# Three moves in a fused attention kernel: beta added to the residual's copy in DRAM, layer 0's product ahead of attention times v, and the projection always in a two-bank tile

## The chip, the core and the metric

The kernel runs on one core of one Trainium2 chip. The metric is the device time of a run in microseconds (us). All runs quoted are "fast" (no disturbed clock). PE is TensorE, DVE is VectorE, ACT is ScalarE, POOL is GpSimd, SP is SyncE; PEld in the profile is PE's weight load. SBUF is the on-chip memory that holds the kernel's tiles, PSUM the one into which PE writes its products (in this program in banks of 128 x 512 floats), DRAM the memory that holds inputs and outputs.

## The reference

The input x holds 128 blocks of 128 x 512 floats. There are two layers, each followed by a layer norm; cut to what matters:

```python
# layer 0: x[b] (128 x 512), adj (128 x 128), bias per row.
# With W1 = W2 = adj the gnn reduces to relu(max over columns of (adj @ x + b)) per row.
x = layernorm(x + L0(x, adj, adj, b0))
# layer 1: 8 heads of 64, masked with adj == 0
q, k, v = split(x @ w_qkv)
attn = softmax(where(adj == 0, -inf, q @ k.T * 64 ** -0.5))
o = (attn @ v) @ w_proj + b_proj
x = layernorm(x + o + layernorm(o) * gamma + beta)
```

## The kernel before

The 128 blocks are worked on in 32 groups of four. A period has two parts: the dense part (q and k of the group, transposed; PE alone sets the pace) and the attention part, in which PE does four times, for one block each: transposes of the softmax weights (`ppt`), scores of the present group (`psc`), the transposes of the next group's x (`ptx`), attention times v of the last group (`pav`), the output projection, a product for v (`pm`/`pd`), and layer 0's product of the group after next (`pa`). Dense products are done in three pieces: a float is split into a high part (rounding on ACT, mask on DVE), a low part and a correction, `x_h`, `x_l`, `x_d`; attention's output likewise into `oh`, `ol`, `od`.

The parts that the change touches:

```python
ps_1 = ctx.enter_context(tc.tile_pool(name="ps_1", bufs=4, space=bass.MemoryType.PSUM))  # one bank each
ps_2 = ctx.enter_context(tc.tile_pool(name="ps_2", bufs=2, space=bass.MemoryType.PSUM))  # two banks each

def conv(b):                       # layer 0's product
    ...
    pa[b] = ps_1.tile([P, D], FP, tag="ps1", name=f"pa_{b}")
    nc.tensor.matmul(pa[b], adjT, xs[b], start=True, stop=True)

def split(key, src, dsts):         # src is ptx or pav, in PSUM
    fh, fl, fd = dsts
    xh = work.tile([P, KC, P], FP, tag="xh", name=f"xh_{key}")
    nc.vector.tensor_scalar(xh.bitcast(I32), src.bitcast(I32), HIGH, None, op0=ALU.bitwise_and)
    hs[key] = fh, xh
    nc.vector.tensor_tensor(fl, src, xh, op=ALU.subtract)        # the last reader of src
    nc.vector.scalar_tensor_tensor(fd, fl.bitcast(FP), -HALF, xh, op0=ALU.mult, op1=ALU.add)

def product(key, two, terms):
    if two:
        pp = ps_2.tile([P, 2, D], FP, tag="ps2", name=f"pp_{key}")
        pm, pd = pp[:, 0, :], pp[:, 1, :]
    else:
        pm = ps_1.tile([P, D], FP, tag="ps1", name=f"pm_{key}")
        pd = ps_1.tile([P, D], FP, tag="ps1", name=f"pd_{key}")
    ...                            # 8 matmuls into pm, 4 into pd

def attention(g, t, starts):       # the order of PE and ACT is that of these places
    for i in range(G):
        u = t + starts[i]
        ...                        # now: group g, last: g - 1, nxt: g + 1, far: g + 2
        last(0.0, transpose_e)
        last(1.0, weights_T)
        now(0.95, scores)
        now(2.1, masked)
        now(3.5, row_max)
        ...
        nxt(2.0, transpose_x)
        nxt(2.5, split_x)
        ...
        u += 2.5
        if g < NG - 1:
            last(0.0, attend)
            u += 1.0
        if i and 0 < g:
            projection((g - 1) * G + i - 1, u)
            u += 2.8
        ...
        last(0.1, heads)
        last(0.8, lambda b: split_high(("o", b)))
        if 0 < g != NG - 1 and i < G - 1:
            dense_step(min(g, NG - 1), i + 1, u)
            u += 2.8
        far(-20.0, load_x)
        far(0.0, conv)
        far(1.0, conv_max)
        ...
```

The order on PE and ACT is given by hand, as these places; that on DVE and POOL is chosen by the scheduler of the program builder.

## Time and profile before

| | before |
|---|---|
| time, median of 3 runs | 2110.77 us (2108.1 to 2110.89) |
| span of the profiled run | 2108.8 us, granted clock 0.992 |
| up to the dense part of group 2 | 141.9 us |
| groups 2 to 29, 28 periods | 1802.5 us, median period 64.31 us, late groups 1.8 us |
| group 30 | 61.5 us |
| from the dense part of group 31 to the end | 102.9 us |

The time is from the first session; the comparison further down has one run more, hence 2110.83 us there. The rows after the second are cut from the trace by the start of the first dense matmul of each group. A "late group" is one whose period is over 0.05 us above the median; the sum is what the 28 periods take over 28 medians (rounded to 0.01 us, so it is good to some 0.2 us). The prediction shows the lines of the profile and how they are read; two groups of the page that it quotes only as numbers are these (line of the program, engine, operation, output and input tile, shapes, count; then busy us and mean ns of one; then idle time ahead of them and what ended most of it):

```profile
L420 ACT ACTIVATE o<-o,sum 128x512 f32<-128x512 f32 x128 | 104.0, 813 | 148.2 <-POOL sum L406 147.7
L360 POOL DMA_DIRECT2D xb<-in_L_gnn_ln_beta_dram x128 | 118.8, 928 | 203.8 <-DMA xb<-x 185.6
```

ACT stands 147.7 us behind small norm steps of POOL, and POOL stands 185.6 us behind loads of the residual (`xb`), because it may add beta to it only when it has landed.

### The profile page before, as it was taken

The page shows a single profiled execution, that of the slowest core. Times are in us where ns is not written, and L with a number is a line of the kernel's source. Part 1 is how long each engine was busy: PE and PEld are TensorE (multiplying, and loading weights), DVE is VectorE, ACT ScalarE, POOL GpSimd, SP SyncE. Part 2 cuts the span into 40 slices and gives each one's busy share as a digit, 9 for nine tenths or more (in the row PEclk, how much of TensorE's full clock was granted, in tenths as well). Part 3 has the DMA queues.
Part 4 walks back from the last instruction along what each step waited for, and adds up shares of the span by engine and source line. Part 5 has one row for each costly group of instructions (what it writes and reads, how often), then busy time and mean ns, then how long its engine had stood idle before and what let it go on. Part 6 is the DMA issues. An engine that isn't in the chain of part 4 may idle for free. (4 is left out here: it accounts for less than half of the span.)

```text
span 2108.8 us, 35003 instructions
## 1 busy us (share of the span) xinstructions
PE 2053.4 (97%) x12033; PEld 1599.1 (76%) x12033; DVE 1613.3 (77%) x2615; ACT 1458.4 (69%) x4130; POOL 734.8 (35%) x1329
## 2 busy tenths in 40 slices
PE   7899999999999999999999999999999999999997
PEld 5677777777777777777777777777777777777775
DVE  7787777887777877778877778777788777788777
ACT  5766676776767766767667677667677676776665
POOL 2123333323433333333234332333332343333345
PEclk9999999999999999999999999999999999999998
DMA  6224444445544345444455443444444444434444
GB/s 186 65 66 125 126 124 108 97 113 131 129 106 110 97 125 127 124 104 99 114 130 129 107 109 97 126 127 124 104 100 114 130 131 108 108 101 109 116 106 115
DMA packets 134433, 240.64 MB, mean 114 GB/s; under 512 B 14704, under 2 KB 18928, under 8 KB 134256
## 3 DMA queue, kind: packets, MB, share of 16 engines
q1 hardware_dynamic: 97680, 172.27, 25.2%
q0 software_dynamic: 36288, 66.08, 18.8%
q8 instruction: 95, 1.56, 0.3%
q14 instruction: 82, 0.67, 0.1%
q10 hardware_dynamic: 288, 0.07, 0.0%
HBM read 138.74 MB, written 67.11 MB: 98 GB/s over the span
## 5 line engine op out<-in xcount | busy, mean ns | idle before, releaser
L317 ACT ACTIVATE e<-e,nmax 128x128 f32<-128x128 f32 x1024 | 396.6, 391 | 3.8 <-DVE nmax L310 3.8
L380 POOL DMA_DIRECT2D xb<-o x124 | 112.9, 910 | 686.9 <-DVE o L385 593.5
L336 ACT COPY eT<-ppt 128x1024 f32<-128x1024 f32 x128 | 129.4, 1011 | 123.6 <-PE ppt L332 123.5
L420 ACT ACTIVATE o<-o,sum 128x512 f32<-128x512 f32 x128 | 104.0, 813 | 148.2 <-POOL sum L406 147.7
L398 POOL TENSOR_TENSOR sum<-sum,mhalf 128x1 f32<-128x1 f32 (+1 forms) x291 | 198.2, 681 | 22.3
L403 POOL TENSOR_SCALAR sum<-sum 128x1 f32<-128x1 f32 x256 | 140.8, 550 | 169.1 <-DVE o L385 167.1
L385 DVE SCALAR_TENSOR_TENSOR o<-o,sum,xb 128x512 f32<-128x512 f32 x128 | 95.7, 747 | 135.0 <-POOL sum L398 131.2
L317 ACT ACTIVATION_READ_ACCUMULATOR e<-e,nmax 128x1 f32 x1024 | 193.9, 189 | 0.0
L391 ACT ACTIVATE square<-o,sum 128x512 bf16<-128x512 f32 x256 | 183.4, 716 | 11.8 <-DVE o L385 9.8
L360 POOL DMA_DIRECT2D xb<-in_L_gnn_ln_beta_dram x128 | 118.8, 928 | 203.8 <-DMA xb<-x 185.6
L412 DVE SCALAR_TENSOR_TENSOR o<-o,sum,gamma_sb 128x512 f32<-128x512 f32 x128 | 95.9, 749 | 100.1 <-ACT square L391 95.3
L397 POOL TENSOR_SCALAR sum<-sum 128x1 f32<-128x1 f32 (+1 forms) x291 | 106.9, 368 | 187.5 <-ACT square L391 174.1
L332 PEld LDWEIGHTS ppt<-ident,e 128*128 128x128 f32 x1024 | 120.6, 142 | 51.8 <-issue 46.6
L302 DVE SCALAR_TENSOR_TENSOR e<-psc,mask 128x1024 f32<-128x1024 f32 x128 | 156.1, 1219 | 3.9 <-PE psc L295 3.9
L326 DVE TENSOR_TENSOR e<-e,sums 128x1024 f32<-128x1024 f32 x128 | 154.8, 1210 | 1.1
L310 DVE TENSOR_REDUCE nmax<-e 128x8 f32<-128x1024 f32 x128 | 154.7, 1209 | 0.0
L295 PE MATMUL psc<-qkT 64*128 64x128 f32 x2048 | 150.3, 286 | 2.8 <-DVE qkT L284 2.7
L170 PE MATMUL pa<-xt,adjT 128*128 128x512 f32 x256 | 133.9, 609 | 12.3 <-PE pd_(15, 1)_9801 L252 0.6
L295 PEld LDWEIGHTS psc<-qkT 64*128 64x128 f32 x2048 | 125.0, 188 | 26.9 <-issue 18.4
L345 PE MATMUL pav<-eT,v 128*64 128x128 f32 x2048 | 140.2, 279 | 2.1 <-ACT eT L336 2.1
L332 PE MATMUL ppt<-ident,e 128*128 128x128 f32 x1024 | 133.7, 274 | 0.0
L345 PEld LDWEIGHTS pav<-eT,v 128*64 128x64 f32 x2048 | 109.2, 136 | 24.8 <-issue 22.1
(4778 smaller groups left out, 5563.5 us busy)
## 6 DMA issues: line engine op xcount, KB each, us to landing
xt<-in_x_dram SPq DMA_DIRECT2D x128, 256.0 KB, 2.8
x<-xt SPq DMA_DIRECT2D x128, 256.0 KB, 3.6
xb<-x SPq DMA_DIRECT2D x128, 256.0 KB, 2.8
xb<-in_L_gnn_ln_beta_dram POOLq DMA_DIRECT2D x128, 256.0 KB, 4.4
o<-in_L_gnn_b_proj_dram SPq DMA_DIRECT2D x128, 256.0 KB, 3.8
out_dram<-o SPq DMA_DIRECT2D x128, 256.0 KB, 3.3
xb<-o POOLq DMA_DIRECT2D x124, 256.0 KB, 3.5
wraw<-in_L_gnn_w_qkv_dram SPq DMA_DIRECT2D x12, 256.0 KB, 4.2
```

Of the source, the lines that this page charges most:

```text
L170: nc.tensor.matmul(pa[b], adjT, xs[b], start=True, stop=True)
L295: nc.tensor.matmul(psc[:, s, hp, :], qkT[hs, hp, i, :], qkT[hs, KC + hp, i, :], start=True, stop=True,)
L302: nc.vector.scalar_tensor_tensor(e, pscs.pop(b).rearrange("p s a m -> p (s a) m"), scale, mask_b, op0=ALU.mult, op1=ALU.add,)
L310: nc.vector.tensor_reduce(nmax, es[b], AX.X, ALU.max, negate=True)
L317: nc.scalar.activation(e[:, j, :], e[:, j, :], AF.Exp, bias=nmax[:, j : j + 1], accum_out=sums[:, j : j + 1],)
L326: nc.vector.tensor_tensor(e, e, sums[:, :, None].to_broadcast([P, H, P]), op=ALU.mult)
L332: nc.tensor.transpose(ppts[b][:, j, :], e[:, j, :], ident)
L336: nc.scalar.copy(eTs[b], ppts.pop(b))
L345: nc.tensor.matmul(pavs[b][s * HD : (s + 1) * HD, hp, :], v[:, h * HD : (h + 1) * HD], eT[:, s * HP + hp, :], start=True, stop=True,)
L391: nc.scalar.activation(square, x, AF.Square, bias=s[:, 0:1], scale=-float(D), accum_out=s[:, 1:2],)
L398: nc.gpsimd.tensor_tensor(s, s, mhalf[:, :n], op=ALU.pow)
L403: nc.gpsimd.tensor_scalar(s[:, 2:3], s[:, 0:1], -1.0 / D, None, op0=ALU.mult)
```

## The change

The intent has three parts, called A, B and C from here on. **A**: layer 0's product moves from the end of a block to just ahead of attention times v. **B**: the projection of a group's first block gets a two-bank tile like the others. **C**: beta is added by a DMA to the residual's copy in DRAM, long before that copy is loaded again, rather than to the loaded copy in SBUF; the last step of the norm moves half a place later.

```diff
--- before.py
+++ after.py
@@ -208,6 +208,10 @@
         x1s[b] = dram.tile([P, D], FP, tag="x1", name=f"x1_{b}")
         nc.sync.dma_start(x1s[b], xs[b])
 
+    def beta_0(b):
+
+        nc.gpsimd.dma_start(x1s[b], row(ln_beta), accum_op=ALU.add)
+
     def transpose_x(b):
         g, i = divmod(b, G)
         pts[b] = ps_1.tile([P, KC, P], FP, tag="ps1", name=f"ptx_{b}")
@@ -352,16 +356,12 @@
         split(("o", b), pavs.pop(b), oTs[b])
 
     def residual(b):
-
         xbs[b] = work.tile([P, D], FP, tag="xb", bufs=3, name=f"xb_{b}")
         nc.sync.dma_start(xbs[b], x1s.pop(b))
 
-    def residual_beta(b):
-        nc.gpsimd.dma_start(xbs[b], row(ln_beta), accum_op=ALU.add)
-
     def project(b):
         parts = [*zip(oTs.pop(b), proj_forms)]
-        product(("o", b), b % G != 0, lambda kc: [(f[:, kc, :], w[:, kc, :]) for f, w in parts])
+        product(("o", b), True, lambda kc: [(f[:, kc, :], w[:, kc, :]) for f, w in parts])
 
     def bias(b):
         os[b] = work.tile([P, D], FP, tag="o", bufs=4, name=f"o_{b}")
@@ -434,7 +434,6 @@
     def normed(b, u, v, w, z):
 
         at(u - 14.0, residual, b)
-        at(u - 10.0, residual_beta, b)
         at(u - 4.0, residual_o, b)
         at(u, stats, b, 1)
         at(v, norm_1, b)
@@ -466,6 +465,10 @@
             nxt(2.5, split_x)
             nxt(3.3 if i == 3 else 5.0, split_high)
             u += 2.5
+            if g + 2 < NG:
+                far(0.0, conv)
+                far(0.9, conv_max)
+                u += 0.9
             if g < NG - 1:
                 last(0.0, attend)
                 u += 1.0
@@ -481,8 +484,6 @@
                 dense_step(min(g, NG - 1), i + 1, u)
                 u += 2.8
             far(-20.0, load_x)
-            far(0.0, conv)
-            far(1.0, conv_max)
             if NG - 1 <= g:
                 v = u + 8.9 if g == NG else u + 12.5 + 2.0 * i
                 normed((g - 1) * G + i, v, v + 1.5, v + 3.1, v + (8.6 if g == NG else 5.6))
@@ -512,12 +513,13 @@
                 v = u + (14.0 + 1.5 * i if g == 0 else (17.0, 21.0, DENSE + 4.0, DENSE + 12.0)[i])
                 at(v, norm_0, b + i)
                 at(v + 1.0, keep_0, b + i)
+                at(v + 25.0, beta_0, b + i)
         for i in range(G):
             if g > 0:
                 at(t + 6.0 + 3.0 * i, weights, (g - 1) * G + i)
             if g > 1:
                 u = t + (3.0, 7.5, 12.0, DENSE + 2.0 if g < NG - 1 else 16.0)[i]
-                normed((g - 2) * G + i, u, u + 3.5, u + 7.0, u + 10.5)
+                normed((g - 2) * G + i, u, u + 3.5, u + 7.0, u + 11.0)
 
 
     for b in range(G):
@@ -531,6 +533,7 @@
         at(u + 4.5, rstd_0, b, 1)
         at(u + 6.0, norm_0, b)
         at(u + 7.0, keep_0, b)
+        at(30.0 + b, beta_0, b)
         at(u + 7.0, transpose_x, b)
         at(u + 8.2 + 0.7 * b, split_x, b)
         at(u + 8.9 + 0.7 * b, split_high, b)
```

## The prediction

> **What bounds the kernel now.** I read the page's engine shares first, then busy time by stretches, then the timeline of one steady period of TensorE (PE) and VectorE (DVE), then the waits of PE. PE leads:
>
> ```profile
> PE 2053.4 (97%) x12033; PEld 1599.1 (76%) x12033; DVE 1613.3 (77%) x2615; ACT 1458.4 (69%) x4130; POOL 734.8 (35%) x1329
> ```
>
> The kernel works on 32 groups of four blocks. From the first matmul of one group's dense part to that of the next the timeline shows 64.3 us for nearly every group, and two neighbouring periods in the view by stretches are equal to the last digit (columns: span, then busy us of PE, PEld, DVE, ACT, POOL, granted clock, DMA share, GB/s):
>
> ```profile
> 1237.00:1301.30 64.30, 63.80 (x379) 49.79 (x377) 49.36 (x81) 44.92 (x129) 22.85 (x41) 1.00 0.45 115
> 1301.30:1365.60 64.30, 63.80 (x379) 49.79 (x377) 49.36 (x81) 44.92 (x130) 22.83 (x41) 1.00 0.45 115
> 1301.90:1329.70 27.80, 27.80 (x121) 22.28 (x120) 14.85 (x28) 20.76 (x55) 15.65 (x30) 1.00 0.48 120
> 1329.70:1365.10 35.40, 34.90 (x255) 26.96 (x254) 33.41 (x51) 23.06 (x72) 7.18 (x11) 1.00 0.43 115
> ```
>
> The reader is to see that PE has no idle time in the dense part (third line) and 0.5 us in the attention part (fourth), where DVE is busy 33.4 of 35.4 us. So time is PE's own work plus what DVE makes it wait in the attention part. The two places are in PE's timeline of that period (start, duration, then in brackets the idle time before):
>
> ```profile
> 1335.33 1.10 PE L252 MATMUL pd_(20, 1)_12966<-w_d,x_d 128*128 128x512 f32 x4
> 1336.83 1.10 PE L170 MATMUL pa<-xt,adjT 128*128 128x512 f32 x2 [0.40 <-PE pd_(20, 1)_12966 L252]
> ...
> 1343.41 1.09 PE L252 MATMUL pd_('o', 76)_13062<-p_d,od 128*128 128x512 f32 x4
> 1344.60 0.47 PE L249 MATMUL pm_(20, 2)_13084<-w_h,x_h 128*128 128x512 f32 x1
> ```
>
> Starts are safer than modelled ends. From pd's start to pa's is 1.50 us; four 128x512 matmuls at the 0.233 us spacing seen between them elsewhere take 0.93, so 0.57 us is a stall. From pd('o', 76) to pm(20, 2) is 1.19 us, so 0.26 us. After each the next start comes 0.08 us late as well (pa's second at 0.504 instead of 0.428; pm's at 0.31 instead of 0.233). Sum: 0.57 + 0.26 + 0.16 = 0.98 us a period. The releaser named is PE's own last matmul, which cannot be the reason: PE does not depend on it. DVE's timeline shows the reason:
>
> ```profile
> 1334.33 0.68 DVE L224 TENSOR_SCALAR xh<-ptx 128x512 int32<-128x512 int32 x1
> 1334.92 1.21 DVE L310 TENSOR_REDUCE nmax<-e 128x8 f32<-128x1024 f32 x1
> 1336.05 0.68 DVE L226 TENSOR_TENSOR x_l<-ptx,xh 128x512 fp32r<-128x512 f32 x1
> ...
> 1343.77 0.68 DVE L226 TENSOR_TENSOR x_l<-ptx,xh 128x512 fp32r<-128x512 f32 x1
> ```
>
> The first x_l ends at 1336.73 and pa starts at 1336.83; the second ends at 1344.45 and pm(20, 2) starts at 1344.60. x_l is the last reader of ptx (transposed x), and the one-bank PSUM pool has four buffers in rotation: in the first block of a period the order of allocation is ptx, pav, pm, pd, pa, so pa gets ptx's bank; in the second ptx, pav, pm('o'), pd('o'), pm(20, 2), so pm gets ptx's bank. The built program's semaphore waits say the same: both wait for DVE's x_l. PE's waits show the first stall once in each of the groups 2 to 29, 28 times, with 0.4 us idle (0.6 where something came late):
>
> ```profile
> PE pa L170 <- PE pd_(21, 1)_13599 L252: 0.4, 1, 0.4
> PE psc L295 <- DVE qkT L284: 2.7, 2, 1.8
> ```
>
> The second line is two extra waits (0.92 us in group 15's scores, 1.8 at the end): the period of group 15 is 65.67 us and of group 7 64.77, so 1.36 + 0.46 = 1.8 us of late arrivals in this run.
>
> **What the Trainium skill says.** "Perfetto Trace Analysis", section Optimization Strategy: consistent bubbles on the engine that should be saturated can mean there is too little SBUF or PSUM for the next tile. The trace agrees: 0.57 us, once a period, 28 times. Same page, Tensor Engine Instruction: the matmul's end is an estimate; agreed, the records overlap (pm's matmuls take 0.40 us and start 0.233 apart), hence I count by starts. "TensorE: Matmul & The Clock Gate", The mechanism: matmuls run in strict program order; so one waiting pa holds everything behind it, as the transposes ppt, which follow at 0.93 us, show. "DMA: Bandwidth & Descriptors", SWDGE vs HWDGE vs iDMA: accumulating in a DMA is for GpSimd-issued DMAs alone; so both versions keep beta's transfer on POOL (0.93 us per issue).
>
> **The change part by part.**
>
> (1) Layer 0's product (pa) ahead of attention times v. I listed the built programs' order on each engine. Per block PE now runs ppt, psc, ptx, pa, pav, projection, dense v. No matmul is added. With (2) the one-bank order is ptx, pa, pav, pm, pd in each of the first blocks: five tiles over four buffers, so pd takes ptx's bank, and later pa takes pm's, pav takes pd's, and so on. DVE's order moves too: xh(ptx), pa's maximum, x_l, then the row maximum (1.21 us), so x_l no longer stands behind it. For the first block, keeping this period's clock: pa at 1332.34 (0.86 long), pav 1333.20, pm 1334.22, pd 1336.2. DVE: xh 1334.33, maximum 1334.92, x_l 1335.5 to 1336.2. In the program pd waits for that maximum, which ends 1335.6: 0.6 us spare. The next ppt starts at 1337.1 instead of 1337.76: the first stall is gone.
>
> (2) Projection always in a two-bank tile. Block 0's projection leaves the one-bank rotation, pm(20, 2) no longer waits for x_l of its own block, and the second stall is gone. The price: its DVE reader waits for the whole product (before: main half only), and it needs one of two two-bank buffers, freed by the copy of ppt to eT. By the same hand-carried clock eT's copy ends at 1340.6, the projection starts 1341.7: spare 1.1 us.
>
> New tight places: DVE's xh of pav ends at 1338.5 instead of 1337.33 (pa's maximum and x_d ahead of it), so ACT makes oh to 1339.15, v to 1339.65, eT to 1340.6. PE wants pa of the second block at 1339.78 (it takes the bank that v's copy frees) and pav at 1340.64: spare 0.1 us and about 0. I expect 0 to 0.1 us lost here. Carrying on through blocks 3 and 4 (DVE full, starts 0.60 us apart for 128x512, 1.13 for 128x1024) finds spares of 0.15 us or more, and the next group's first dense matmul at 1365.04, against 1366.0 now: 0.96 us.
>
> (3) Beta half a period early. 128 DMAs of 256 KB into the residual's SBUF copy go, 128 into its DRAM copy come; POOL issues as many (0.93 us each, 118.8 us). It is off PE's path. What moves: POOL no longer waits 185.6 us for the residual to land before issuing beta, and its small norm steps come sooner, so ACT waits less (147.7 us behind POOL now). ACT is not the bound; the worth is fewer late qkT, of which this run had 1.8 us. DRAM traffic grows by 128 x 256 KB read and written, at a DMA share of 0.45: hidden.
>
> Sum: 28 x 0.96 = 26.9, plus 1.8 late arrivals = 28.7; less 28 x 0.05 for the tight place = 27.3. Start (79 us) and end (103 us) keep PE's order but for the two-bank projections, whose later reader may cost up to 1 us: 26 to 28. 2110.8 - 27.5 = **2083.3 us**.
>
> **The rivals.** (a) Wait changed for another: DVE is 94% busy in the attention part and ACT's oh comes 1.2 us later; were pa of the second block or pav to wait 0.3 us per period, gain falls by 8: 2092. For: spare is about 0. Against: DVE's sequence is gapless in both, so no later chain forms. (b) DVE becomes the bound: its 33.4 of 35.4 us would leave 2.0 us, the change takes 0.96 of it; should it bind in every group the gain is halved: 2097. Against: the dense part leaves DVE 13 of 27.8 us idle to catch up. (c) The DRAM accumulate comes late or slows the loads: no gain or a loss, 2110 or more. Against: half a period, some 30 us, against landings of 2.8 to 4.4 us. (d) More than expected: all of PE's stalls gone in the start and the end as well (9.3 + 6.5 us at the start hang on ACT's normalising, untouched). Not expected.
>
> **Range and chances.** The most that is in it is the removal of every steady stall and late arrival, 29 us: 2081; with luck at the ends 2077. Rival (a) in full and a little of (b): 2094. Over 2% faster means below 2068.6, which needs 13 us more than the stalls hold: 0.02. Slower needs rival (c) badly: 0.01.
>
> **What would show it.** Right: periods of 63.3 to 63.4 us; no wait of pa or of pm(g, 2) on x_l; POOL without beta's waits for the residual; pp_('o', 4k) in place of pm and pd. Wrong: a wait of the second block's pa on v's copy, or of pav on eT, of over 0.1 us in every period; idle time of PE in the dense part; POOL waiting at the new accumulate.

## The result, and the profile after

The changed kernel took 2082.05 us (median of 4 runs, 2080.48 to 2082.71) beside 2110.83 us (4 runs, 2108.1 to 2111.79) for the kernel before. The ratio is 0.9865, with a 95% interval of 0.9848 to 0.9882: 1.35% less. A ratio here is always the mean time of one kernel's fast runs over that of the other's fast runs of the same rounds, so it is not quite the ratio of the medians.

The page's first line for the engines, and one period in the view by stretches (columns as in the prediction; its neighbour has the same 63.47):

```profile
PE 2042.2 (98%) x12033; PEld 1591.0 (76%) x12033; DVE 1622.0 (78%) x2615; ACT 1451.7 (70%) x4130; POOL 701.5 (34%) x1329
```

```profile
1286.40:1349.87 63.47, 63.47 (x377) 49.54 (x376) 49.68 (x81) 44.71 (x128) 22.19 (x41) 1.00 0.52 117
```

The same work is done (12033 matmuls, 2615 DVE instructions). A period is 63.47 us rather than 64.30, and PE is now busy in all of it. The timeline of PE at the place that the prediction showed, now of the changed kernel (start, duration, idle time before it in brackets where the profile shows any):

```profile
1316.47 0.66 PE L220 MATMUL ptx<-ident,xt 128*128 128x128 f32 x4
1316.96 1.02 PE L170 MATMUL pa<-xt,adjT 128*128 128x512 f32 x2
...
1320.91 1.09 PE L256 MATMUL pd_(20, 1)_12960<-w_d,x_d 128*128 128x512 f32 x4
1321.84 1.04 PE L336 MATMUL ppt<-ident,e 128*128 128x128 f32 x8
...
1323.90 0.66 PE L220 MATMUL ptx<-ident,xt 128*128 128x128 f32 x4
1324.45 1.12 PE L170 MATMUL pa<-xt,adjT 128*128 128x512 f32 x2
...
1328.49 1.10 PE L256 MATMUL pp_('o', 76)_13053<-p_d,od 128*128 128x512 f32 x4
1329.43 0.40 PE L253 MATMUL pm_(20, 2)_13076<-w_h,x_h 128*128 128x512 f32 x1
```

After pd_(20, 1) the next start comes 0.93 us later, where before it came after 1.50 us. After the projection's last four matmuls pm_(20, 2) starts 0.94 us later, where before it was 1.19 us. Both stalls are gone. One small new one is there: the two matmuls of the second pa last 1.12 us in sum where those of the first last 1.02, and its start is 0.55 us after ptx's, not 0.49. So that place costs 0.16 us a period. ACT's timeline tells what it waits for:

```profile
1323.28 0.62 ACT L240 CAST oh<-xh_('o', 76)_12976 128x512 fp32r<-128x512 f32 x1 [2.90 <-DVE xh_('o', 76)_12976 L228]
1323.81 0.59 ACT L284 ACTIVATE v<-pm_(20, 1)_12959 128x512 f32<-128x512 f32 x1
1324.30 1.01 ACT L340 COPY eT<-ppt 128x1024 f32<-128x1024 f32 x1
```

The copy of v ends at 1324.40 and pa, which takes the bank of pm_(20, 1), starts at 1324.45. The copy stands behind the rounding of oh, which comes late because DVE now does pa's maximum first. DVE's timeline in the second block:

```profile
1326.77 0.68 DVE L228 TENSOR_SCALAR xh<-ptx 128x512 int32<-128x512 int32 x1
1327.37 0.68 DVE L174 TENSOR_REDUCE rm<-pa 128x1 f32<-128x512 f32 x1
1327.97 0.68 DVE L230 TENSOR_TENSOR x_l<-ptx,xh 128x512 fp32r<-128x512 f32 x1
1328.57 1.21 DVE L314 TENSOR_REDUCE nmax<-e 128x8 f32<-128x1024 f32 x1
```

x_l, which frees ptx's bank, is now ahead of the 1.21-us row maximum, not behind it. Nothing in the diff orders this; the scheduler did it when pa's maximum came to stand earlier. The move does a second thing, which shows when the program is built from the kernel's text again: the banks go round differently. Before, pa took ptx's bank in the first block and pm_(20, 2) in the second. In the changed kernel ptx's bank goes to the next block's ptx, pd_(20, 1) takes pa's and pm_(20, 2) takes that of pd_(20, 1); in the trace pm_(20, 2) waits for no semaphore at all. So there no product of the same block depends on x_l any more, wherever it stands on DVE. The runs do not separate the two effects in the changed kernel.

The groups of the page that answer to ACT's and POOL's of before:

```profile
L213 POOL DMA_DIRECT2D x<-in_L_gnn_ln_beta_dram x128 | 115.6, 910 | 325.1 <-DMA x<-xt 308.3
...
L420 ACT ACTIVATE o<-o,sum 128x512 f32<-128x512 f32 x128 | 103.9, 811 | 33.5 <-POOL sum L406 33.4
```

POOL waits more than before for the transfer that beta's add depends on (308.3 us rather than 185.6), but now the wait is for the residual's store to DRAM, and it comes when POOL has nothing else to do that matters: ACT's wait behind POOL's norm steps fell from 147.7 to 33.4 us. The price is in the page's DMA lines (queue, count, size of one, median us from issue to landing; for after also HBM traffic), first of before, then of after:

```profile
xb<-in_L_gnn_ln_beta_dram POOLq DMA_DIRECT2D x128, 256.0 KB, 4.4
```

```profile
x<-in_L_gnn_ln_beta_dram POOLq DMA_DIRECT2D x128, 256.0 KB, 6.4
HBM read 138.74 MB, written 100.66 MB: 115 GB/s over the span
```

An accumulate into DRAM lands after 6.4 us, one into SBUF after 4.4; 128 x 256 KB = 33.5 MB more are written (67.11 MB before), and loads of x land after 4.6 us (2.8 before). What is read stays at 138.74 MB. All of it is far from the time that it has: in the profile after, from the landing of beta's add to the load of the same copy it is 81 to 149 us (blocks 3 to 127, transfers paired in their order).

Where the 28.9 us between the two profiled spans (2108.8 and 2079.9) come from:

| stretch | before | after | difference |
|---|---|---|---|
| up to group 2 | 141.9 | 144.0 | +2.1 |
| 28 medians of the period | 28 x 64.31 | 28 x 63.47 | -23.5 |
| late groups (group 7: 0.47, group 15: 1.36) | 1.8 | 0 | -1.8 |
| group 30 | 61.5 | 60.9 | -0.6 |
| from group 31 to the end | 102.9 | 97.9 | -5.0 |

In 0.4 us of the first row and of that of group 30 only the cut differs: where pa stands just ahead of the dense part (the kernels without A, groups 2 to 30), the record of the first dense matmul starts over pa's second one, and the next start comes 0.64 us later rather than 0.23. So some +1.7 and -0.2 us are left there. The median periods are not touched by this.

### The profile page after: what moved, and what is told of

It is laid out like the page before. It is cut to its first block, busy times and chain, and to the rows that moved or that the text cites. A ratio compares the mean times of both kernels' runs of the same rounds, so it can differ in the third digit from the quotient of the medians.

```text
span 2079.9 us, 35025 instructions
## 1 busy us (share of the span) xinstructions
PE 2042.2 (98%) x12033; PEld 1591.0 (76%) x12033; DVE 1622.0 (78%) x2615; ACT 1451.7 (70%) x4130; POOL 701.5 (34%) x1329
## 3 DMA queue, kind: packets, MB, share of 16 engines
HBM read 138.74 MB, written 100.66 MB: 115 GB/s over the span
## 5 line engine op out<-in xcount | busy, mean ns | idle before, releaser
L380 POOL DMA_DIRECT2D xb<-o x124 | 120.2, 970 | 358.4 <-DVE o L385 342.1
L397 POOL TENSOR_SCALAR sum<-sum 128x1 f32<-128x1 f32 (+1 forms) x291 | 100.5, 345 | 391.5 <-ACT square L391 379.5
L213 POOL DMA_DIRECT2D x<-in_L_gnn_ln_beta_dram x128 | 115.6, 910 | 325.1 <-DMA x<-xt 308.3
L398 POOL TENSOR_TENSOR sum<-sum,mhalf 128x1 f32<-128x1 f32 (+1 forms) x291 | 185.6, 638 | 22.5
L403 POOL TENSOR_SCALAR sum<-sum 128x1 f32<-128x1 f32 x256 | 157.5, 616 | 41.1 <-DVE o L385 35.6
L420 ACT ACTIVATE o<-o,sum 128x512 f32<-128x512 f32 x128 | 103.9, 811 | 33.5 <-POOL sum L406 33.4
```

What stands on the lines that cost most here:

```text
L398: nc.gpsimd.tensor_tensor(s, s, mhalf[:, :n], op=ALU.pow)
L403: nc.gpsimd.tensor_scalar(s[:, 2:3], s[:, 0:1], -1.0 / D, None, op0=ALU.mult)
```

## The experiments

The theory at the start of the experiments: PE's two steady stalls are waits for x_l, which frees a one-bank buffer late because the row maximum is ahead of it on DVE; part A takes both away, part B adds nothing to A, and part C takes away the late groups alone. The main rival: each of A and B takes one stall away (0.65 and 0.34 us a period, so some 18 and 9 us), and the gain is their sum. Where the texts use letters, M is this theory and R the rival that a run is set against. A further rival: beta's path through POOL is on the critical path in every period. Runs 1 to 4 shared one chip and the runs of before (2112.15 us, 9 runs), 5 to 8 another (2110.34, 9 runs), 9 and 10 a third (2111.59, 7 runs). All were correct, of state fast, and timed in 5 rounds. The segments are from the profile of each, as in the table above.

| run | median us | ratio to before [95%] | to group 2 | median period | late groups, sum | group 30 | end |
|---|---|---|---|---|---|---|---|
| before | 2110.83 | | 141.9 | 64.31 | 1.8 | 61.5 | 102.9 |
| after | 2082.05 | 0.9865 [0.9848, 0.9882] | 144.0 | 63.47 | 0 | 60.9 | 97.9 |
| 1: A | 2089.10 | 0.9891 [0.9878, 0.9905] | 144.3 | 63.48 | 4.6 | 61.1 | 100.4 |
| 2: B | 2102.51 | 0.9955 [0.9942, 0.9967] | 143.6 | 63.97 | 4.2 | 61.3 | 100.9 |
| 3: C | 2103.89 | 0.9963 [0.9949, 0.9977] | 142.3 | 64.31 | 0 | 61.6 | 97.6 |
| 4: A + B | 2089.76 | 0.9892 [0.9878, 0.9905] | 143.8 | 63.48 | 3.5 | 60.9 | 101.8 |
| 5: before, row maximum later | 2094.84 | 0.9931 [0.9918, 0.9943] | 141.8 | 63.78 | 2.0 | 61.0 | 100.4 |
| 6: after, v ahead of oh | 2078.61 | 0.9849 [0.9835, 0.9862] | 144.2 | 63.31 | 0 | 60.0 | 100.2 |
| 7: after without beta | 2080.57 | 0.9862 [0.9848, 0.9875] | 142.9 | 63.47 | 0 | 60.9 | 97.8 |
| 8: A + C | 2081.06 | 0.9867 [0.9854, 0.9881] | 142.7 | 63.47 | 0 | 61.1 | 97.6 |
| 9: as 6, steady groups alone | 2078.80 | 0.9850 [0.9834, 0.9867] | 143.2 | 63.31 | 0 | 60.9 | 99.4 |
| 10: after, again | 2081.32 | 0.9857 [0.9843, 0.9872] | 143.1 | 63.47 | 0 | 60.9 | 97.9 |

### 1. Part A alone

```diff
+            if g + 2 < NG:
+                far(0.0, conv)
+                far(0.9, conv_max)
+                u += 0.9
             if g < NG - 1:
                 last(0.0, attend)
                 u += 1.0
 ...
-            far(0.0, conv)
-            far(1.0, conv_max)
```

> Only layer 0's product ahead of attention times v; projection's tiles and beta as before. Theory M (the steady stalls come from DVE's splitting of the transposed x freeing its PSUM bank late, and moving the product also moves its maximum and with it the last reader x_l ahead of the row maximum on DVE): both stalls go, though the second is nominally the other part's: period 64.31 to about 63.5 us, total about 2086 us (2083 to 2089). Rival R (each part removes its own stall): only the first stall goes, 0.64 us x 28 = 18 us, 2093 us, and the second, 0.26 + 0.08 us before pm(g, 2), is still there.

Measured: 2089.10 us, ratio 0.9891. The time is at the edge of what the theory expected, but the period answers clearly: 63.48 us, that of the changed kernel to 0.01. Moving pa clears both stalls. In the program built from this kernel, pd_(20, 1) takes pa's bank and pm_(20, 2) still takes ptx's; so the first stall goes with the bank, and the second because x_l is ahead of the row maximum. What keeps the time above the changed kernel's is not in the steady period: 11 late groups, 4.6 us in sum, which the kernel before had less of (group 15 alone is 2.0 us late), and an end of 100.4 us rather than 97.9.

### 2. Part B alone

```diff
-        product(("o", b), b % G != 0, lambda kc: [(f[:, kc, :], w[:, kc, :]) for f, w in parts])
+        product(("o", b), True, lambda kc: [(f[:, kc, :], w[:, kc, :]) for f, w in parts])
```

> Only the projection always in two-bank tiles. M and R agree: the second stall goes (0.34 us x 28 = 9.5 us), the first (0.57 + 0.08 us before layer 0's product) stays: period 63.97 us, 2101 us (2098 to 2104). If DVE is the bound of the attention part instead, the first stall grows by what the second loses and the time stays at 2110.

Measured: 2102.51 us, ratio 0.9955. The period falls by 64.31 - 63.97 = 0.34 us, exactly the second stall (0.26) with its late second start (0.08). PE's waits (us in total, times, longest) still show the first, once a group; one of the lines:

```profile
PE pa L170 <- PE pd_(16, 1)_10419 L252: 0.6, 1, 0.6
```

28 x 0.34 = 9.5 us of steady gain, of which 2.4 us are lost again to more late groups. B by itself works as intended.

### 3. Part C alone

```diff
+    def beta_0(b):
+        nc.gpsimd.dma_start(x1s[b], row(ln_beta), accum_op=ALU.add)
 ...
-        at(u - 10.0, residual_beta, b)
 ...
+                at(v + 25.0, beta_0, b + i)
 ...
-                normed((g - 2) * G + i, u, u + 3.5, u + 7.0, u + 10.5)
+                normed((g - 2) * G + i, u, u + 3.5, u + 7.0, u + 11.0)
 ...
+        at(30.0 + b, beta_0, b)
```

> Only beta added in DRAM half a period early. M: both stalls stay, period 64.31 us; the late arrivals of group 7 and 15 (1.8 us) go, the end gains up to 5 us because POOL and ACT are less late there, the start loses about 1 us to the added traffic: 2104 to 2109 us. If beta were what matters, most of the 28.8 us would come here: 2085.

Measured: 2103.89 us, ratio 0.9963, at the lower edge of what was expected. The steady period is unchanged at 64.31: beta's path is not on the critical path of a normal period, which ends the further rival. But no group is late, and the end is 5.3 us shorter. So C is worth 6.7 us in the profile (2108.8 to 2102.1), far more than the 1.8 us of late groups that the prediction saw (1.5 us of it are put down to chance below). How a late group comes about is in the timelines of the kernel before around group 15, of POOL, ACT, DVE and PE in turn:

```profile
1005.39 0.94 POOL L360 DMA_DIRECT2D xb<-in_L_gnn_ln_beta_dram  x1 [4.46 <-issue]
...
1007.33 0.19 POOL L406 TENSOR_TENSOR sum<-sum 128x1 f32<-128x1 f32 x1
```

```profile
1007.55 0.82 ACT L420 ACTIVATE o<-o,sum 128x512 f32<-128x512 f32 x1 [3.39 <-POOL sum L406]
```

```profile
1008.88 0.69 DVE L284 TENSOR_TENSOR qkT<-qkT,pd_(15, 11)_9717 128x512 f32<-128x512 f32 x1 [4.00 <-ACT qkT L280]
```

```profile
1009.62 0.49 PE L295 MATMUL psc<-qkT 64*128 64x128 f32 x4 [0.92 <-DVE qkT L284]
```

POOL stands idle 4.46 us ahead of beta's issue, at 1005.39. Only the first part of this is the wait for the residual, which landed at 1002.87. In the last 2.5 us POOL waited for nothing that the profile shows (hence "issue"); 0.5 us from such a landing to the issue is usual. This delay is there once in each of the eleven profiles with beta, 2.45 to 2.48 us, and always ahead of POOL's 114th transfer; run 7, with 124 transfers in all, has none. Why is open. With beta in its old place it falls in group 15, which is 1.4 to 2.0 us late in all five profiles; with C the 114th transfer is an add to DRAM in group 14, and no group is late. Group 7 is the plain case: there the residual landed 4.2 us after its issue (the median is 2.8), and POOL issued beta 0.6 us after that.

The small norm steps behind the issue end at 1007.5; ACT's last norm step waits for them, and behind that step in ACT's order is the last copy of q and k, which DVE and then the scores need. In these timelines each engine keeps the order of its program, so a late issue of beta's add reaches PE over three engines. With beta added elsewhere, POOL's norm steps have nothing slow ahead of them.

### 4. Parts A and B together

```diff
 (the edits of runs 1 and 2)
```

> Both PE-side parts, beta as before. M: as e1 in the periods (63.5 us), since the projection's tile has nothing left to remove: 2086 us, within 2 us of e1, and 2 to 5 us over the whole change, which is beta's share. R: e1's and e2's gains add up, 18 + 9.5, so 2083, and e4 is 9 us faster than e1.

Measured: 2089.76 us, ratio 0.9892, beside 0.9891 for A alone, and the same period of 63.48 us. With A, B is worth nothing that shows; the additive rival, which gave it 9 us, is refuted. From this run to the changed kernel (which adds C) it is 7.7 us at the medians, though of different chips, and 5.7 us by the two ratios, whose intervals just overlap; in the profiles 7.5: late groups 3.5, the end 3.9 (of which 1.3 are the last product's clock, see 9 and 10). The text had expected 2 to 5 us.

### 5. The kernel before, with the row maximum placed later

This leaves PE's order as it was and changes DVE's only: x_l is no longer behind the row maximum.

```diff
-            now(3.5, row_max)
+            now((3.5 if not 0 < g < NG - 1 else (5.0, 8.5, 8.5, 8.5)[i]), row_max)
```

> The kernel before, with PE's order, PSUM tiles and beta untouched; only the row maximum's place in the plan is later in the steady groups, so that DVE's x_l, the last reader of ptx, comes ahead of it in every block. Theory M (the bank is released late because DVE's x_l stands behind the row maximum): the first stall goes (0.64 us), the second stays at about 0.2 us since PE arrives 0.64 us earlier: period about 63.6 to 63.8 us, total 2092 to 2098. Rival P (what counts is that PE issues layer 0's product elsewhere): both stalls stay, 2110 us.

Measured: 2094.84 us, ratio 0.9931, a gain of 15.5 us at the medians without moving a matmul. PE's and then DVE's timeline:

```profile
1325.91 1.09 PE L252 MATMUL pd_(20, 1)_12964<-w_d,x_d 128*128 128x512 f32 x4
1326.88 1.10 PE L170 MATMUL pa<-xt,adjT 128*128 128x512 f32 x2
```

```profile
1326.10 0.68 DVE L226 TENSOR_TENSOR x_l<-ptx,xh 128x512 fp32r<-128x512 f32 x1
...
1328.50 1.21 DVE L310 TENSOR_REDUCE nmax<-e 128x8 f32<-128x1024 f32 x1
```

From pd's start to pa's it is 0.97 us rather than 1.50, and pa starts 0.10 us after x_l's end. This shows that the wait is for x_l and that the row maximum ahead of it made it late; "PE pd" as the releaser was only the last thing that the profile saw end. The second stall is still there (the period is 63.78: 0.53 us less of 0.98), because that x_l still comes late for pm_(20, 2): it ends at 1334.50, and pm_(20, 2) starts at 1334.65. No row maximum is ahead of it there any more; DVE works up to it without a gap.

### 6. The changed kernel with v's copy ahead of oh

The one tight place left in the steady period is pa of the second block, behind v's copy, behind oh on ACT. For the first block of each group oh is put later:

```diff
-            last(0.8, lambda b: split_high(("o", b)))
+            last(2.0 if i == 0 else 0.8, lambda b: split_high(("o", b)))
```

> The changed kernel, with ACT's copy of the first block's v ahead of its copy of oh, which waits for DVE. M: the tight place (pa of the second block late by 0.06 us and its second matmul by 0.10 us, released by that copy of v) goes: period 63.47 to 63.30 us, total 2082 to 2077.5 us. Rival: the 0.17 us are a fixed cost of going from transposes to this product: no change, 2082.

Measured: 2078.61 us (2077.08 to 2078.88), ratio 0.9849. ACT's and PE's timeline of the same group:

```profile
1318.43 0.60 ACT L284 ACTIVATE v<-pm_(20, 1)_12959 128x512 f32<-128x512 f32 x1 [0.73 <-PE pm_(20, 1)_12959 L254]
1320.61 0.62 ACT L240 CAST oh<-xh_('o', 76)_12976 128x512 fp32r<-128x512 f32 x1 [1.57 <-DVE xh_('o', 76)_12976 L228]
```

```profile
1321.22 0.66 PE L220 MATMUL ptx<-ident,xt 128*128 128x128 f32 x4
1321.71 1.02 PE L170 MATMUL pa<-xt,adjT 128*128 128x512 f32 x2
```

pa now comes 0.49 us after ptx and lasts 1.02 us. The period is 63.31 us, 0.16 less, 28 times, which is the 4.5 us by which the 28 periods in sum became shorter (1777.1 to 1772.6). It also confirms the size of the stalls: 64.31 - 63.31 = 1.00 us against 0.98 counted in the prediction. All five runs (2077.08 to 2078.88) are below those of runs 7 and 8 on the same chip (from 2079.77).

### 7. The changed kernel without any beta

The reference's beta is all zeros, so leaving it out gives a correct result here; it is an experiment, not a version.

```diff
-                at(v + 25.0, beta_0, b + i)
 ...
-        at(30.0 + b, beta_0, b)
```

> The changed kernel without any of beta's transfers (beta is zero in these inputs, so the result is still right here, though it is not the function in general). M: they are hidden where they are now; periods stay at 63.47 us, start and end move by under 2 us: 2080 to 2082. Rival T (the added DRAM traffic costs something): periods shorter too, 2077 or less.

Measured: 2080.57 us (2079.77 to 2081.91), ratio 0.9862 [0.9848, 0.9875], against 0.9865 and 0.9857 for the changed kernel. Period, late groups and end are the same. So the 128 accumulating transfers, with 33.5 MB read (138.74 against 105.19) and 33.5 MB written to HBM, and POOL's 115.6 us of issuing cost nothing that can be told from zero.

### 8. Parts A and C, without B

```diff
-        product(("o", b), True, lambda kc: [(f[:, kc, :], w[:, kc, :]) for f, w in parts])
+        product(("o", b), b % G != 0, lambda kc: [(f[:, kc, :], w[:, kc, :]) for f, w in parts])
```

> The changed kernel with the projection's tile choice undone (one-bank tiles for the first block of a group again). M: nothing lost, 63.47 to 63.5 us a period, 2082 us (within 2 us). Rival R (each part removes its own stall): the second stall comes back, 0.34 us x 28, 2091.

Measured: 2081.06 us, ratio 0.9867 [0.9854, 0.9881]; the whole change has 0.9865. B is redundant beside A with C too.

### 9 and 10. The best version, and the changed kernel again

Run 6 had a longer end (100.2 us against 97.9) and waited there 0.5 us for oh of block 119. In run 9 oh is put later in the steady groups alone:

```diff
-            last(0.8, lambda b: split_high(("o", b)))
+            last(2.0 if i == 0 and g < NG - 2 else 0.8, lambda b: split_high(("o", b)))
```

> The changed kernel with ACT's rounding copy of attention's output delayed behind v's copy for the first block of a group, as in the run that moved v first, but in the steady groups alone. That run gained 28 times 0.16 us in the steady groups (1777.1 to 1772.6 us) and had 2.3 us more after the last group's dense part began, of which 0.8 us are waits for oh that the delay itself can explain and 1.5 us a half-speed last product. Theory: the steady gain stays and the ends keep the changed kernel's time: 4 to 5 us under the changed kernel of the same job, 2076.5 to 2078.5. Rival: the gain at the steady place is taken back by later waits at the end, so no better than the earlier run: 2078 to 2080.

> The changed kernel itself, unaltered, for a comparison with the run above on the same chip: 2080 to 2083, and no late group in its profile if beta's move is what removes them; one or more late groups of 0.4 us or more if their absence was chance.

Measured on one chip: 2078.80 us (2078.03 to 2082.26) for run 9 and 2081.32 us (2080.61 to 2082.58) for the changed kernel. The medians differ by 2.5 us, the means of four runs by 2.0, short of the 4 to 5 expected at the optimistic end; one of run 9's four runs was as slow as the other kernel's. In the profile the waits at the end are gone (the last product starts 83.81 us after the first dense matmul of group 31, as in the changed kernel), and the steady period is 63.31. The 1.5 us by which its end is still longer (99.4 against 97.9) lie in the last product alone, which ran at half the clock in this profile. So runs 6 and 9 are the fastest versions, some 2 to 3.5 us under the changed kernel; between the two no difference shows. The changed kernel's second profile again has no late group: of the seven profiles with C or without beta none has one, of the five with beta's add in its old place all have some.

The half-speed end needs its evidence. Before and after, the last product on PE starts after a wait of 1.74 us for oh. In PE's timeline its matmuls start 0.43 us apart before (2094.58, 2095.01 and so on) and 0.23 us apart after (2066.92, 2067.15), both behind the same wait. From that product's start to the end of the span the twelve profiles take two values only: 14.0 to 14.1 us in six (after, 3, 5, 7, 8, 10) and 15.4 to 15.6 in six (before, 1, 2, 4, 6, 9). The two groups cut across the edits (5 has no C, 6 and 9 have it), so this 1.5 us is put down to chance, the clock's phase, and to no part of the change. That is argued and not shown: but for the changed kernel, whose two profiles agree (14.1 us), there is one profile for each. The Trainium skill, "TensorE: Matmul & The Clock Gate", Part 1, says that the window over which activity is judged runs freely, so that the same kernel falls into it differently from run to run; the two values fit that, and no run here shows the window itself.

## Why the prediction was right, and which of its terms were off

The time predicted was 2083.3 us, measured 2082.05; the range held. The main mechanism held too, but two terms of the sum were mis-sized, in opposite directions, so that the closeness is in part luck.

**The bound and the stalls: right.** PE's waits for x_l were named as the reason behind a releaser that could not be it. Run 5 shows it directly for the first stall, and run 6 gives 1.00 us for the stalls of 0.98. The 0.96 us of the sum are a second count, carried by hand, and 1366.0 is in no line: the record of that matmul, pp_(21, 4), starts at 1365.60 over pa's second one, and 1366.0 is the start after it (1366.23) less one spacing.

**(1) and (2), which part does what: half right.** The prediction noted that pa's move carries x_l ahead of the row maximum, and gave the first stall to A and the second to B. The first holds. The second is cleared by A as well (run 1: the full 0.83 us), so B, though it works alone (run 2: 0.34 us), adds nothing (runs 4 and 8). The sum was untouched by this, as both were to be made at once. The step that failed is to have worked out each part's effect on the old order only, not B's after A. Its order of banks was wrong in one place, too: in the program built from the changed kernel pd takes pa's bank, not ptx's, and ptx's goes to the next ptx. The wait that it named for pd, pa's maximum, fits the right one, so the timing was not hurt.

**The tight place: named, too small.** "Pa of the second block [...] takes the bank that v's copy frees" is where the loss is. It was allowed 0.05 us a period and costs 0.16 (run 6), of which the visible wait is 0.06 and the rest is that pa's second matmul starts late as well. This makes the steady gain 28 x 0.84 = 23.5 us in place of 28 x 0.91 = 25.5. The prediction had counted such a late second start for the old stalls and forgot it for the new one. The sign given for a failure (a wait of over 0.1 us there in every period) was thus half met: rival (a) is at work, at half its assumed size.

**(3), C's worth: the term that was most off.** It was put at the 1.8 us of late groups in one profile. Those went. But the profile of before had a wait of the same kind near its end, counted in the text as "1.8 at the end" and left out of the sum: the scores of group 31 waited 1.81 us for qkT, and PE ran at half speed after it. The view by stretches of before, just after that wait (the granted clock is the third number from the end), and PE's timeline of before and then of after:

```profile
2036.00:2040.00 4.00, 4.00 (x33) 3.22 (x27) 2.97 (x4) 2.93 (x6) 0.24 (x2) 0.57 0.66 161
```

```profile
2034.83 0.49 PE L295 MATMUL psc<-qkT 64*128 64x128 f32 x4 [1.81 <-DVE qkT L284]
...
2036.44 1.97 PE L332 MATMUL ppt<-ident,e 128*128 128x128 f32 x8
```

```profile
2010.62 1.09 PE L336 MATMUL ppt<-ident,e 128*128 128x128 f32 x8
```

The granted clock is 0.57 there, and eight transposes take 1.97 us rather than 1.09. The 5.0 us that the end became shorter are about 2.0 of this wait, 1.5 of the slower clock after it, and 1.5 of the last product's clock, put down to chance. The prediction had 0 to 1 us of loss for start and end together. PE's wait itself is there in before, 4 and 5, in no profile with C, but not in 1 and 2 either. What leads to it is a wait of DVE (us in total, times, longest):

```profile
DVE o L412 <- DMA xb<-o: 4.7, 1, 4.7
```

DVE's norm step stood until 2028.81 for the transfer that adds o to the residual in `xb`, which took 7.1 us (3.5 at the median); POOL had issued it 0.3 us after beta's add to the same buffer had landed. The last copies of q and k queue behind that norm step. All five profiles with beta in its old place have this wait: 4.6 to 6.7 us where it reaches PE, 2.9 us in runs 1 and 2, where it doesn't. In run 3 and the changed kernel the step waits under 0.02 us. So C takes the chain away; what it is worth at the end rests on one profile for each kernel, though the medians agree (run 3: 2103.89 against 2112.15; run 4 to the changed kernel 7.7 us).

**The start: no term, and +2.1 us in the two profiles.** It is unresolved: the changed kernel's own two profiles have 144.0 and 143.1 us, and the twelve lie between 141.8 and 144.3. In the profile of before the first wait for x_h in group 1 is 6.5 us, in that of after 4.1, while pa waits 2.3 us more for a load of x; where one wait shrinks another grows. 0.4 us of the 2.1 is the cut, as said under the table.

**The signs.** Periods of "63.3 to 63.4" were 63.47. No wait of pa or pm on x_l, the two-bank projection and the busy dense part came as said. "POOL waiting at the new accumulate" was given as a sign of being wrong; it waits 308.3 us there and it doesn't matter (run 7). It was a badly chosen sign: what counts is whether work that others need stands behind the wait. Rivals (b) and (c) are refuted: PE is busy in all of the period, DVE in 49.7 of 63.5 us, and beta's transfers can't be told from none. Of (c)'s figures three were off without harm: an add to DRAM lands after 6.4 us, not 2.8 to 4.4; it has 81 us or more, not some 30; and HBM shows 33.5 MB more written but none more read. Rival (d), a gain in the ends, is the one that came true in part.

So the predicted 27.5 us and the measured 28.8 are close because two misses cancel: 2.0 us less in the steady part, and 3.5 us more in the start, group 30 and the end together (+2.1 - 0.6 - 5.0), of which 1.5 are put down to chance. The prediction's own terms, 27.3 less up to 1, would have given 26.3 to 27.3, not 26 to 28.

## What to carry to other kernels

When an engine waits for itself in the profile, look for the buffer it is about to write, and for the last reader of what lay in it: putting that short reader ahead of a long instruction on its own engine (run 5, one line changed) gave over half of what the whole change gave. Look also at which tile gets that buffer in the new order: a move changes both. Work out the parts of a change one after the other and not each against the old kernel, because a second remedy for the same wait is worth nothing. A wait for a transfer costs by what stands behind it in program order: move the transfer to where nothing that others need is behind it, even if it then waits longer (308.3 us here, at no cost).

## What the Trainium skill lacked or had wrong

- "TensorE: Matmul & The Clock Gate", Part 4: PE-mode transpose, says that the full clock doesn't engage for its transpose mode. In these traces 128x128 f32 transposes start 0.109 us apart at a granted clock of 1.00, and 0.213 us apart where the half-speed stretch above shows 0.57, so they follow the clock as other matmuls do. Whether these are the page's transpose mode the trace doesn't tell, and whether transposes alone would bring the full clock no run shows.
- The same page, section "Wait — 56ns, not 53.3ns?", gives a start-to-start time of 215.7 ns for 512 columns at full clock, with no word on types there. No page gives one for fp32r: such matmuls start 234 ns apart here, with a weight load for each. The f32 ones (pa) start 430 ns apart.
- "DMA: Bandwidth & Descriptors" says who may issue an accumulating DMA, but not what it costs: 256 KB land 6.4 us after issue in DRAM and 4.4 us in SBUF here (3.5 us where the source is in SBUF too), and the issue holds POOL 0.91 to 0.93 us.
- No page read says that the profile may name the waiting engine's own last instruction as releaser when a PSUM buffer's reader on another engine is the cause (0.57 us, 28 times in the kernel before; run 5).
- No page was found that names the delay of POOL's 114th transfer: 2.45 to 2.48 us, once in each of eleven profiles.
